# A schedule in pairs for the image parts of a four-layer model on one core, with some of its evictions moved between engines

## The chip, the core and the metric

The kernel runs on one core of one Trainium2 chip. The metric is device time in microseconds (us), the median over runs. The kernel before takes 21348.91 us (three runs, 21327.56 to 21384.39).

## The reference

Eight images of 56 x 56 pixels and 192 channels pass through four residual layers in float32; each layer normalizes its input by groups first (`_gn`).

```python
def _gn(v, G=32, eps=1e-5):
    ...
x = x + _L0_conv_ref(_gn(x), ...)   # gated Toeplitz products along rows and columns
x = x + _L1_conv_ref(_gn(x), ...)   # attention in shifted windows of 7 x 7, 6 heads of 32
x = x + _L2_conv_ref(_gn(x), ...)   # depthwise 3 x 3 convolution
x = x + _L3_conv_ref(_gn(x), ...)   # selective scan in four directions
```

The core of each:

```python
# layer 0
p, q, v = silu(x @ p_w.T + p_b), silu(x @ q_w.T + q_b), silu(x @ v_w.T + v_b)
out = (p * (toeplitz_rows(q * v) + toeplitz_columns(q * v))) @ o_w.T + o_b
# layer 1
attn = softmax(q * scale @ k.T + bias + mask); out = (attn @ v) @ proj_w.T + proj_b
# layer 3: DI = 384 channels, N = 16 states, K = 4 directions, L = 3136 positions
xi, z = split(x @ in_proj_w.T); xc = silu(depthwise_conv(xi)); z = silu(z)
dts, Bs, Cs = split(einsum('bkdl,kcd->bkcl', xs, x_proj_w))
delta = softplus(einsum('bkrl,kdr->bkdl', dts, dt_w) + delta_bias)
h[l] = exp(delta[l] * A) * h[l-1] + delta[l] * u[l] * B[l];  y[l] = sum over N of h[l] * C[l] + D * u[l]
out = (layernorm(sum over the directions of y) * z) @ out_proj_w.T
```

## The kernel before

**Ahead of the loop.** Some 3290 us prepare everything: the products q * v of layer 0 for all images, the Toeplitz products along both axes, and the whole *front* of image 0.

**A front** is what one image needs before its scan can run. It is a Python generator that calls five stages in order: `gate` (the rest of layer 0: the projection p with its Silu, transposes on TensorE, the output projection), `attention` (layer 1), `conv2` (layer 2), `inner` (layer 3's input projection, its convolution and its Silu) and `steps` (the projections to delta, B and C). Each `yield` ends a *piece*, a short run of instructions; the yield says how many PSUM banks the piece holds, how many the next one needs, and after which time a load will have landed. A front has 1144 pieces.

**The loop of pairs.** The scan is cut into chunks of 448 positions. A chunk has three blocks of 128 channels and 16 states, taken two states at a time: a *pair*. An image has 4 directions x 7 chunks x 3 x 8 = 672 pairs; all images, 5376. The order is written out by hand (`manual_schedule`). For one pair: GpSimd multiplies delta * u by B into a ring buffer (`inject`, L1102); ScalarE computes exp(delta * A) into a double-buffered PSUM tile ps_a (`decay`, L1119, two instructions); VectorE scans (`scan`, L1128); GpSimd (even pairs) or VectorE (odd pairs) multiplies by C into one of four hc buffers (`times_c`, L1134); TensorE adds up over the states in PSUM (`add_up`, ps_y, L1149); ScalarE copies a few columns of state (L1109, L1141). Once in eight pairs VectorE adds ps_y into ysum (`sums`, L1159 and L1161).

**Front beside scan.** While image b is scanned, `Parts.step`, called once per pair, resumes pieces of the front of image b + 1, and of `finish` (layer 3's normalization and output for chunks that are complete). The planner keeps an estimated time for each engine (`self.t`) and the estimated cost of every piece, logged by `Meter` when a piece first runs, from fixed prices per instruction and column. `fits` lets a piece in if, by these estimates, VectorE would not have to wait more than 0.2 us for its input and ScalarE and TensorE stay below limits that depend on the next scans. A piece that doesn't fit waits for the next pair, and each such wait adds 3 us to what it is allowed:

```python
t, at, grace = dict(self.t), entry.ready, 3.0 * entry.waits
for engine, cost in entry.costs[entry.at]:
    if engine == "D" and at > t["D"] + limit["D"] + grace:
        return False
    at = t[engine] = max(t[engine], at) + cost
return all(t[e] <= max(limit[e] + grace, self.t[e]) for e in "AE")
```

So a front goes ahead as fast as it fits, and the next front is added as soon as the last one is done. There is one point at which it is forced: before the first chunk of the next image is loaded (16 pairs before the image's end), the planner drains the front until the delta of that chunk has been made (`made`).

All pieces of fronts and of finish share two PSUM banks (`bank`, tile ps_f), the scan has the others. Every engine runs its instructions in the order in which they were put in, and so does the DMA queue on SyncE, which carries nearly all transfers.

**What the change touches in `attention` and `steps`.** In `attention`, for every quarter of a row of windows, the scores of heads 4 and 5 and the values v share one PSUM bank: ScalarE copies v out (L688) and VectorE reads the scores with scale and bias (`biased`, L662); a reduction for the maximum follows (L691), then the exponentials (L694) and a reciprocal (L699). In `steps`, for each of 14 chunks and 3 channel blocks, two banks hold delta for the two directions of a scan order; ScalarE evicts both with their bias (L976), and then takes the Softplus of the whole chunk with its table loads (L980, L428).

Other lines that are named below: L546 to L566 belong to `gate`, L823 to L835 are conv2's convolution and its evictions, L854 loads the rows for inner's convolution, L912 is that convolution and L922 its eviction, L961 and L971 are the matmuls of `steps`. In the first execution of a front (for image 0) all lines appear as L83, the helper that records the costs.

Of the kernel before, what the change touches and what calls it, by code (L numbers as in the profile page):

```python
# [17 lines left out]
ALU = mybir.AluOpType  # L18
# [21 lines left out]
WP = W + 2  # L40
RUN = 8 * WP
SLOT = NG * (CH + 1) + HALF


class Meter:
# [43 lines left out]
def model(ctx: ExitStack, tc: tile.TileContext, a: dict, out: bass.AP):  # L89
# [300 lines left out]
    with (  # L390
# [44 lines left out]
        nc.vector.tensor_reduce(Dsum, Ds, axis=AX.X, op=ALU.add)  # L435


        meter, costs = Meter(tc.nc), {}
        made = set()


# [129 lines left out]
        def attention(b):  # L571
# [52 lines left out]
            for wh in range(H // WS):  # L624
# [27 lines left out]
                for q in range(4):  # L652
                    kind = 2 * (wh == 7) + (q == 3)

                    def scores(p, hh, t):
                        row = slice(hh * HD, (hh + 1) * HD)
                        nc.tensor.matmul(
                            p[:PT_, t * PT_ : (t + 1) * PT_], qk[row, t, q, :], qk[row, 2 + t, q, :], start=True, stop=True
                        )

                    def biased(p, hh):
                        nc.vector.scalar_tensor_tensor(  # L662
                            S[:, 2 * hh : 2 * hh + 2, :],
                            p[:PT_, : 2 * PT_].rearrange("p (t m) -> p t m", t=2),
                            HD**-0.5,
                            bmask[:, kind, 2 * hh : 2 * hh + 2, :],
                            ALU.mult,
                            ALU.add,
                        )


                    yield 0, 2
                    p0, p1 = bank(), bank()
                    for t in range(2):
                        scores(p0, 0, t)
                        scores(p1, 1, t)
                    yield 2, 0
                    biased(p0, 0)
                    biased(p1, 1)
                    yield 0, 1  # L680
                    p = bank()
                    for t in range(2):
                        scores(p, 2, t)
                    pv = p[:PT_, 2 * PT_ : 2 * PT_ + C]
                    for k in range(2):
                        nc.tensor.matmul(pv, xw[:, k, q, :], w_qkv[:, k, 2 * C :], start=k == 0, stop=k == 1)
                    yield 1, 0
                    nc.scalar.copy(v, pv)  # L688
                    biased(p, 2)
                    mx, sm = mxs[:, 0], mxs[:, 1]  # L690
                    nc.vector.tensor_reduce(mx, S, axis=AX.X, op=ALU.max, negate=True)  # L691
                    yield 0, 0
                    for e in range(6):
                        nc.scalar.activation(  # L694
                            S[:, e, :], S[:, e, :], AF.Exp, bias=mx[:, e : e + 1], accum_out=sm[:, e : e + 1]
                        )
                        if e == 2:
                            yield 0, 0
                    nc.vector.reciprocal(sm, sm)  # L699
                    yield 0, 0  # L700
                    for e in range(6):
                        nc.scalar.activation(S[:, e, :], S[:, e, :], AF.Copy, scale=sm[:, e : e + 1])  # L702
                        if e == 2:
                            yield 0, 0
                    for g in range(2):
                        yield 0, 1
                        p = bank()
                        for e in range(3):
                            nc.tensor.transpose(  # L709
                                p[:PT_, e * PT_ : (e + 1) * PT_], S[:, 3 * g + e, :], ident[:PT_, :PT_]  # L710
                            )
                        yield 1, 0
                        nc.scalar.copy(
                            ST[:, 3 * g : 3 * g + 3, :].rearrange("p a m -> p (a m)"), p[:PT_, : 3 * PT_]
                        )
                    yield 0, 1
                    p = bank()
                    for t in range(2):
                        for hh in range(3):
                            h = 3 * t + hh  # L720
                            nc.tensor.matmul(
                                p[hh * HD : (hh + 1) * HD, t * PT_ : (t + 1) * PT_],
                                v[:, h * HD : (h + 1) * HD],
                                ST[:, 2 * hh + t, :],
                                start=True,
                                stop=True,
                            )
                    yield 1, 0
                    nc.scalar.copy(oT[:, :, q, :], p[:CP, : 2 * PT_].rearrange("p (t m) -> p t m", t=2))
# [212 lines left out]
        def steps(b):  # L942
# [11 lines left out]
            for n, (o, j) in enumerate(todo):  # L954
                tok = slice(j * CH, (j + 1) * CH)
                if n + 1 < len(todo):
                    load_x(n + 1)
                yield 0, 1
                p = bank()
                for d in range(ND):  # L960
                    nc.tensor.matmul(p[:, :CH], w_x[:, o, d, :], xc[:, n % 2, d, :], start=d == 0, stop=d == ND - 1)  # L961
                yield 1, 0
                nc.scalar.copy(rc[:, n % 2, :], p[:, :CH])
                nc.sync.dma_start(out=bc_d[o][b][:, tok], in_=rc[64:, n % 2, :])
                for d in range(ND):
                    yield 0, 2
                    held = []
                    for s in range(2):
                        row = slice(32 * s, 32 * s + R)
                        held.append(bank())  # L970
                        nc.tensor.matmul(  # L971
                            held[s][:, :CH], w_dt[row, o, d * 128 : (d + 1) * 128], rc[row, n % 2, :], start=True, stop=True
                        )
                    yield 2, 0
                    for s in range(2):
                        nc.scalar.activation(  # L976
                            dl[:, s, d, :], held[s][:, :CH], AF.Identity, bias=dt_b[:, 2 * o + s, d : d + 1]
                        )
                yield 0, 0
                nc.scalar.activation(dl, dl, AF.Softplus)  # L980
                usual_functions()
                for s in range(2):
                    nc.sync.dma_start(out=dl_d[2 * o + s][b][:, :, tok], in_=dl[:, s])
                made.add((b, o, j))
            yield 0, 0

        def front(b):
            yield from gate(b)
            yield from attention(b)
            yield from conv2(b)  # L990
            yield from inner(b)
            yield from steps(b)

        def finish(b, j):

# [168 lines left out]
        class Parts:  # L1164
# [4 lines left out]
            def __init__(self):  # L1169
                self.clients = []  # L1170
                self.t = dict.fromkeys("PADE", 0.0)

            def run(self, engine, cost, *after):
                self.t[engine] = max(self.t[engine], 0.0, *after) + cost
                return self.t[engine]

            def add(self, work, name):
                entry = Entry(work, costs.setdefault(name, []))
                self.clients.insert(0 if name != "front" else len(self.clients), entry)
                return entry  # L1180

            def fits(self, entry, limit):
                if entry.at >= len(entry.costs):
                    return True
                t, at, grace = dict(self.t), entry.ready, 3.0 * entry.waits
                for engine, cost in entry.costs[entry.at]:
                    if engine == "D" and at > t["D"] + limit["D"] + grace:
                        return False
                    at = t[engine] = max(t[engine], at) + cost
                return all(t[e] <= max(limit[e] + grace, self.t[e]) for e in "AE")  # L1190

            def resume(self, entry):
                got = log_of(entry.work, entry.costs) if entry.at == len(entry.costs) else next(entry.work, None)
# [10 lines left out]
            def step(self, limit, only=None):  # L1204
                old = [e for e in self.clients if e.held]
                for entry in old + [e for e in self.clients if e not in old]:
                    if only is not None and entry is not only and not entry.held:
                        continue
                    while entry in self.clients:
                        if entry.held and entry not in old:  # L1210
                            break
                        if entry.needs + sum(e.held for e in self.clients if e is not entry) > 2:
                            break
                        if not self.fits(entry, limit):
                            entry.waits += 1
                            break
# [3 lines left out]
                        self.resume(entry)  # L1220

        class Entry:
            def __init__(self, work, costs):
                self.work, self.costs = work, costs
                self.at = self.held = self.needs = self.waits = 0
                self.ready = 0.0

# [32 lines left out]
        with tc.manual_schedule():  # L1260
# [31 lines left out]
            ending, anything = None, dict.fromkeys("ADE", 1e9)  # L1292
            for g, (i, d, k) in enumerate(pairs):
                b, slot, j = chunks[i]
                if ahead_of not in parts.clients and b_next < B:
                    ahead_of = parts.add(front(b_next), "front")
                    b_next += 1
# [53 lines left out]
                times_c(last)  # L1351
            for g in (last - 1, last):
                add_up(g)
            while parts.clients:
                parts.step(anything)
            sums(i, d)
# [105 lines left out]
```

## Time and profile before

| | |
|---|---|
| median of the runs | 21348.91 us (21327.56 to 21384.39) |
| profiled execution, its own time | 21337.26 us |
| its span on the core | 21335.4 us |
| mean granted TensorE clock | 0.885 |
| first to last scan of the loop (L1128) | 3288 to 21296 us |
| gate to steps of the front of image 4 | 10065 to 12310 us |
| scan (L1128), mean of one | 2.02 us |
| GpSimd's inject (L1102) and times_c (L1134), mean of one | 1.77 us |
| VectorE's times_c (L1134), mean of one | 1.09 us |
| one exponential of ScalarE (L1119) | 0.64 us |
| eviction of delta by ScalarE (L976), mean of one | 0.63 us |

The profile is of one execution. PE is TensorE (matmuls), PEld its weight loads, DVE VectorE, ACT ScalarE, POOL GpSimd, SP SyncE. Busy times are summed over instructions; matmuls overlap, so a busy PE is not a full one. A row such as "DVE hc L1134 <- PE ps_y L1149" in the list of waits says that the VectorE instruction of line 1134 that writes hc was ready to go but for the TensorE instruction of line 1149, with the total, the number of times and the longest wait in us.

### The profile page before, as it was taken

What the parts mean: (1) busy time and instruction counts of PE and PEld (TensorE: products, weight loads), DVE (VectorE), ACT (ScalarE), POOL (GpSimd) and SP (SyncE); (2) the same over time, 40 slices, a digit from 0 to 9 for tenths busy, and PEclk for the clock granted to TensorE, in tenths of its full rate; (3) what the DMA queues carried; (4) which work ended last, traced back from release to release, by engine and by line L of the source; (5) the groups of instructions that cost most, each with busy time, mean ns of one, the idle gap of its engine ahead of it and who ended that gap; (6) DMA issues with size and microseconds to landing.
All of it is one profiled execution on the core that took longest, in us unless ns stands there. A gap on an engine that the chain in (4) does not pass through costs nothing. (4 is left out here: it accounts for less than half of the span.)

```text
span 21335.4 us, 204096 instructions
## 1 busy us (share of the span) xinstructions
PE 17278.2 (81%) x59420; PEld 8930.3 (42%) x59420; DVE 15942.8 (75%) x12633; ACT 12339.9 (58%) x31627; POOL 15616.3 (73%) x9378
## 2 busy tenths in 40 slices
PE   8878658878887788878987898879877987787777
PEld 4666524433443344433543354335433443333333
DVE  2432207986798679977897779867987789689998
ACT  3111235766666666757675757666666666575555
POOL 1222206977888778867897778878887788699999
PEclk9988768988998889888998899889988999888888
DMA  4776565456545655475546654565447544754444
GB/s 99 180 179 161 123 189 158 135 171 206 168 135 152 214 160 150 127 205 188 151 138 182 206 154 134 167 210 169 145 138 219 174 143 136 218 177 147 135 133 128
DMA packets 2562886, 3470.49 MB, mean 163 GB/s; under 512 B 932463, under 2 KB 2514897, under 8 KB 2530931
## 3 DMA queue, kind: packets, MB, share of 16 engines
q1 hardware_dynamic: 2456772, 3253.90, 51.3%
q10 hardware_dynamic: 86016, 86.71, 1.8%
q0 software_dynamic: 18976, 116.82, 1.6%
q8 instruction: 473, 7.75, 0.2%
q14 instruction: 649, 5.31, 0.1%
HBM read 2822.68 MB, written 634.11 MB: 162 GB/s over the span
## 5 line engine op out<-in xcount | busy, mean ns | idle before, releaser
L1149 PE MATMUL ps_y<-hc,ident_sb 128*128 128x448 f32 x21504 | 9984.7, 602 | 831.0 <-POOL hc L1134 757.0
L1102 POOL TENSOR_TENSOR ring<-du,bm 128x896 f32<-128x896 f32 x5376 | 9438.2, 1770 | 723.1 <-ACT ring L1109 367.5
L1119 ACT ACTIVATE ps_a<-delta,A_logs_sb 128x449 f32<-128x449 f32 x10752 | 6859.4, 638 | 357.1 <-DVE ring L1128 100.5
L1149 PEld LDWEIGHTS ps_y<-hc,ident_sb 128*128 128x128 f32 x21504 | 4308.3, 210 | 5153.0 <-issue 3638.6
L1134 POOL TENSOR_TENSOR hc<-ring,cm 128x896 f32<-128x896 f32 x2688 | 4757.6, 1770 | 2013.9 <-DVE ring L1128 991.2
L1128 DVE TENSOR_TENSOR_SCAN ring<-ps_a,ring 128x898 f32<-128x898 f32 x2688 | 5423.3, 2018 | 826.0 <-ACT ps_a L1119 719.9
L1128 DVE TENSOR_TENSOR_SCAN ps_a<-ps_a,ring 128x898 f32<-128x898 f32 x2688 | 5426.9, 2019 | 612.1 <-ACT ps_a L1119 552.9
L1134 DVE TENSOR_TENSOR hc<-ps_a,cm 128x896 f32<-128x896 f32 x2688 | 2934.4, 1092 | 1017.2 <-PE ps_y L1149 789.8
L1141 ACT COPY state<-ps_a 128x2 f32<-128x2 f32 x2687 | 425.9, 159 | 2813.2 <-DVE hc L1134 2805.1
L279 POOL COPY tm<-tr 112x2688 f32<-112x2688 f32 x96 | 458.7, 4800 | 1117.2 <-DMA tr<-ext 646.7
L1109 ACT COPY ring<-state 128x2 f32<-128x2 f32 x4608 | 822.9, 179 | 516.8 <-POOL hc L1134 515.9
L312 PE MATMUL ps_tz<-tzx,tm 112*112 112x112 f32 x4608 | 927.1, 370 | 189.2 <-POOL tm L279 181.1
L1085 POOL TENSOR_TENSOR du<-delta,xcd 128x448 f32<-128x448 f32 x672 | 657.0, 978 | 496.8 <-DMA xcd<-xc 496.8
L312 PEld LDWEIGHTS ps_tz<-tzx,tm 112*112 112x112 f32 x4608 | 870.5, 202 | 238.6 <-POOL tm L279 189.1
L316 DVE COPY tzx<-ps_tz 112x448 f32<-112x448 f32 x576 | 356.4, 622 | 744.6 <-PE ps_tz L312 705.2
L709 PE MATMUL ps_f<-ident_sb,slab 98*98 98x98 f32 x1344 | 336.9, 324 | 596.2 <-ACT slab L702 596.0
L1141 ACT COPY state<-ring 128x2 f32<-128x2 f32 x2688 | 504.2, 188 | 474.6 <-DVE ring L1128 459.5
L83 PE MATMUL ps_f<-slab 96*32 96x448 f32 (+7 forms) x2432 | 600.2, 554 | 166.7 <-DMA slab<-pad 76.2
L241 ACT ACTIVATE sl<-ps_qv 128x384 f32<-128x384 f32 x600 | 293.0, 490 | 755.7 <-PE ps_qv L240 612.1
L242 DVE TENSOR_TENSOR qv<-sl 128x576 f32<-128x576 f32 (+1 forms) x200 | 206.8, 1037 | 572.5 <-ACT sl L241 556.6
L709 PEld LDWEIGHTS ps_f<-ident_sb,slab 98*98 98x98 f32 x1344 | 200.9, 155 | 1009.3 <-ACT slab L702 794.2
L546 PE MATMUL ps_f<-ident_sb,slab 112*96 112x112 f32 x4704 | 538.4, 270 | 98.8 <-DVE slab L554 46.3
(223 smaller groups left out, 16977.5 us busy)
## 6 DMA issues: line engine op xcount, KB each, us to landing
bm<-bc SPq DMA_DIRECT2D x1792, 448.0 KB
cm<-bc SPq DMA_DIRECT2D x1792, 448.0 KB
xcd<-xc SPq DMA_DIRECT2D x840, 224.0 KB
dl<-slab SPq DMA_DIRECT2D x224, 672.0 KB
delta<-dl SPq DMA_DIRECT2D x224, 672.0 KB
slab<-pad SPq DMA_DIRECT2D x504, 232.0 KB
o<-tzx POOLq DMA_DIRECT2D x192, 588.0 KB, 12.8
slab<-x SPq DMA_DIRECT2D x280, 336.0 KB
```

The costliest lines, as they stand in the source:

```text
L83: return f(*args, **kw)
L312: nc.tensor.matmul(po[:, c, :], t[:, c2 + c, :], x[:, :, c1 + c2 + c], start=True, stop=True)
L546: nc.tensor.matmul(p[:CP, t * TT : (t + 1) * TT], ot[:, n % 2, i, t, c % 2 * CP : c % 2 * CP + CP], ident[:TT, :TT], start=i == 0, stop=i ...
L709: nc.tensor.transpose(p[:PT_, e * PT_ : (e + 1) * PT_], S[:, 3 * g + e, :], ident[:PT_, :PT_])
L1085: nc.gpsimd.tensor_mul(du[:, 0, :], deltas[i][:, d, 1 : CH + 1], xcs.pop((i, d)))
L1102: nc.gpsimd.tensor_mul(hs[:, :, tokens(i)[0]], dus[i, d].to_broadcast([128, NG, CH]), bms[i, k])
L1109: nc.scalar.copy(in_ring(g)[:, :, tokens(i)[1]], src)
L1119: nc.scalar.activation(dA[:, n, :], deltas[i][:, d, at : at + CH + 1], AF.Exp, scale=negA[:, slot, d, c : c + 1])
L1128: nc.vector.tensor_tensor_scan(h, dA, hs, 0.0, ALU.mult, ALU.add)
L1134: (nc.gpsimd if on_pool(d, k) else nc.vector).tensor_mul(hc, h[:, :, tokens(i)[0]], cms[i, k])
L1141: nc.scalar.copy(states[i][:, d, NG * k : NG * k + NG], h[:, :, tokens(i)[2]])
L1149: nc.tensor.matmul(yps[i, d][:, :CH], ident, hcs[g][:, n, :], start=k + n == 0, stop=k + n == NP + NG - 2)
```

## The change

The change has three parts.

1. The fronts follow a schedule counted in pairs. `PER_FRONT = 676` pairs are given to a front. `shares` divides them among the pieces: for each stage it sums the logged costs by engine, weights them by `ROOM` (pairs per us of TensorE, VectorE and ScalarE work), takes the largest of the three sums or a third of the number of pieces as the stage's share, and splits that among its pieces by their weighted cost. `late` is the number of pairs by which a front is behind its schedule. A front's piece that holds no bank isn't resumed while the front is more than 1.5 pairs ahead, and its grace in `fits` is its lateness (not below zero) in place of 3 us per wait. Pieces that hold a bank, and those of `finish`, keep the old rule.
2. Of the two banks of delta in `steps`, ScalarE evicts the first as before, and VectorE the second (`tensor_scalar`, adding the bias).
3. In `attention`, `biased(p, 2)` on VectorE is issued ahead of ScalarE's copy of v from the same bank.

```diff
+ROOM = {"E": 0.8, "D": 2.2, "A": 0.7}
+PER_FRONT = 676
...
                     yield 1, 0
+                    biased(p, 2)
                     nc.scalar.copy(v, pv)
-                    biased(p, 2)
...
                     yield 2, 0
-                    for s in range(2):
-                        nc.scalar.activation(
-                            dl[:, s, d, :], held[s][:, :CH], AF.Identity, bias=dt_b[:, 2 * o + s, d : d + 1]
-                        )
+                    nc.scalar.activation(dl[:, 0, d, :], held[0][:, :CH], AF.Identity, bias=dt_b[:, 2 * o, d : d + 1])
+                    nc.vector.tensor_scalar(
+                        dl[:, 1, d, :], held[1][:, :CH], dt_b[:, 2 * o + 1, d : d + 1], None, ALU.add
+                    )
...
         def front(b):
-            yield from gate(b)
-            yield from attention(b)
-            yield from conv2(b)
-            yield from inner(b)
-            yield from steps(b)
+            log = costs["front"]
+            for stage in (gate, attention, conv2, inner, steps):
+                if b == 0:
+                    stages.append(len(log))
+                yield from stage(b)
+
+        def shares():
+
+            log, at, share = costs["front"], stages + [len(costs["front"])], []
+            for lo, hi in zip(at, at[1:]):
+                sums = [{e: sum(c for f, c in piece if f == e) * per for e, per in ROOM.items()} for piece in log[lo:hi]]
+                whole = max(len(sums) / 3, *(sum(piece[e] for piece in sums) for e in ROOM))
+                total = sum(sum(piece.values()) for piece in sums)
+                share += [whole * sum(piece.values()) / total for piece in sums]
+            done = [0.0]
+            for v in share:
+                done.append(done[-1] + v / sum(share))
+            return done
...
             def __init__(self):
                 self.clients = []
                 self.t = dict.fromkeys("PADE", 0.0)
+                self.pair, self.done, self.fronts = 0, shares(), -1
...
             def add(self, work, name):
-                entry = Entry(work, costs.setdefault(name, []))
+                entry = Entry(work, costs.setdefault(name, []), name == "front")
+                self.fronts += entry.paced
...
                 t, at, grace = dict(self.t), entry.ready, 3.0 * entry.waits
+                if entry.paced and not entry.held:
+                    grace = max(0.0, self.late(entry))
...
+            def late(self, entry):
+                return self.pair - PER_FRONT * (self.fronts + self.done[entry.at])
...
                         if entry.needs + sum(e.held for e in self.clients if e is not entry) > 2:
                             break
+                        if entry.paced and not entry.held and only is None and self.late(entry) < -1.5:
+                            break
                         if not self.fits(entry, limit):
...
             for g, (i, d, k) in enumerate(pairs):
                 b, slot, j = chunks[i]
+                parts.pair = g
```

More of the change, by code (lines that the diff above doesn't have):

```diff
@@ L435, in model @@
         nc.vector.tensor_reduce(Dsum, Ds, axis=AX.X, op=ALU.add)
-        meter, costs = Meter(tc.nc), {}
+        meter, costs, stages = Meter(tc.nc), {}, []
         made = set()
@@ L1222, in model, with __init__ @@
         class Entry:
-            def __init__(self, work, costs):
-                self.work, self.costs = work, costs
+            def __init__(self, work, costs, paced):
+                self.work, self.costs, self.paced = work, costs, paced
                 self.at = self.held = self.needs = self.waits = 0
@@ L1353, in model @@
                 add_up(g)
+            parts.pair = 2 * len(pairs)
             while parts.clients:
```

## The prediction

> **What bounds the kernel now.** I read the page first for the busy shares, then cut the span into the stages of one image's front, because the 21 ms hold regimes with different limits.
>
> ```profile
> PE 17278.2 (81%) x59420; PEld 8930.3 (42%) x59420; DVE 15942.8 (75%) x12633; ACT 12339.9 (58%) x31627; POOL 15616.3 (73%) x9378
> DVE  2432207986798679977897779867987789689998
> POOL 1222206977888778867897778878887788699999
> ```
>
> No engine is full on the mean. In the 40 slices GpSimd and VectorE are full only in the last five or so, where no front is left; before that they rise and fall with the image. The page's chain of waits covers too little of the span to say more. So: busy time by stage for the front of image 4 (gate, attention, conv2, inner, steps, in order), and last a stretch of image 7 with no front beside it.
>
> ```profile
> 10065.00:10561.00 496.00, 453.61 (x1732) 260.66 (x1731) 409.07 (x314) 284.96 (x659) 396.14 (x240) 0.96 0.58 161
> 10561.00:11344.00 783.00, 651.60 (x2337) 321.13 (x2335) 738.41 (x614) 572.88 (x1804) 704.98 (x421) 0.91 0.42 130
> 11344.00:11513.00 169.00, 111.08 (x408) 40.91 (x408) 132.13 (x121) 67.67 (x174) 104.17 (x62) 0.84 0.62 171
> 11513.00:11932.00 419.00, 326.40 (x1138) 143.15 (x1138) 296.11 (x188) 253.32 (x563) 309.36 (x184) 0.86 0.74 226
> 11932.00:12310.00 378.00, 313.09 (x787) 141.63 (x788) 267.13 (x173) 283.73 (x570) 285.61 (x173) 0.85 0.58 189
> 19600.00:20800.00 1200.00, 872.62 (x1770) 373.51 (x1769) 1148.39 (x722) 670.68 (x1775) 1198.49 (x720) 0.87 0.41 135
> ```
>
> The columns are length, then PE, PEld, DVE, ACT, POOL. The same windows for the scan's line (one scan is one pair) give 138, 258, 39, 114 and 100 pairs, and 444 in the last. Without a front a pair takes 1200/444 = 2.70 us, GpSimd is full and VectorE is busy 1148/444 = 2.59 us of it. A front's 649 pairs take 2245 us where 649 x 2.70 = 1754 would do: 491 us extra. I split that by VectorE. Its own front work (busy less 2.59 per pair) is 52, 71, 31, 1 and 9 us, 164 in all. The rest is its idle time beyond the 0.116 per pair of the free stretch: gate 71, attention 14, conv2 32, inner 110, steps 99, together 326 us. That idle is what a schedule can win. What ends it, by the waits over the whole stretch of the fronts (us in total, times, longest), and then over conv2's 169 us:
>
> ```profile
> DVE hc L1134 <- PE ps_y L1149: 779.0, 480, 11.1
> DVE ps_a L1128 <- ACT ps_a L1119: 513.5, 313, 10.0
> DVE ring L1128 <- ACT ps_a L1119: 408.0, 150, 4.6
> ```
>
> ```profile
> DVE slab L834 <- PE ps_f L823: 33.3, 11, 10.3
> ```
>
> First, VectorE waits for TensorE to free an hc buffer; second, for ScalarE's exponentials. Both engines run in order, so a front's piece that waits holds the pairs up. One case, in order of time:
>
> ```profile
> 4714.05 4.16 PE L912 MATMUL ps_f<-slab 96*32 96x448 f32 x24 [4.23 <-DMA slab<-pad]
> ...
> 4719.94 1.09 DVE L1134 TENSOR_TENSOR hc<-ps_a,cm 128x896 f32<-128x896 f32 x1 [6.64 <-PE ps_y L1149]
> ```
>
> The inner convolution was put into TensorE's queue before its rows had landed; the sums behind it came late, and VectorE stood for 6.6 us.
>
> **The schedule.** The shares follow from the planner's prices (its bookkeeping, not chip times). Gate: 84 projections and 84 output matmuls at 0.60 and 336 transposes at 0.18 make 161 TensorE us, x 0.8 = 129.5. Attention: 559 pieces / 3 = 186. conv2: 25.6 VectorE us x 2.2 = 56. Inner: 108 TensorE us x 0.8 = 86. Steps, with half the evictions moved: 104.7 ScalarE us x 0.7 = 73. Sum 531.7, scaled to 676 pairs: 165, 237, 71, 110, 93, against 138, 258, 39, 114, 100 now. So only gate and conv2 get room; the other three are asked to run slightly denser than they run unpaced. Before, the last front ends at pair 4534 of 5376 (stage positions counted against scans); paced it ends near 7 x 676 = 4732, still with a free last image.
>
> Gate: its 71 us of idle scaled with density, 71 x 138/165 = 59: -12 us a front. TensorE is busy 454 of 496 us here, so density is what hurts.
> Attention: 14 x 258/237 = 15: +1.
> conv2: 33.3 us of its idle is one wait, the eviction at L834 for a convolution that waits for padded rows. By the prices the 14 convolutions come about 3.4 pairs apart instead of little over one, so rows ordered two ahead have some 19 us to land. I take 28 of the 32 us off.
> Inner: the convolution's share is 1.9 pairs a step against about 1.4 now; of the 54.6 us that VectorE waits there for ps_y I take a fifth, -11; the rest at 114/110 gives +4. Net -7.
> Steps: 99 x 100/93 = 106: +7.
> Grace: a piece that doesn't fit gets 3 us more for each pair it waits; a paced one gets its lateness instead. Behind a load of 8 us the old rule issues after one pair, the new one after two if the front is on time. About eleven such waits a front stall TensorE or VectorE; each can win up to one pair (2.7 us) or, when the front is late by 6 or more, lose as much. So between -30 and +30; I take -10, since gate and conv2 leave it on time and the others don't.
>
> **Delta's banks.** 42 of 84 evictions a front leave ScalarE and come to VectorE, with no DMA moved.
>
> ```profile
> L976 ACT ACTIVATE slab<-ps_f,dt_b_sb 128x448 f32<-128x448 f32 x84 | 48.6, 627 | 21.3 <-PE ps_f L971 21.1
> L316 DVE COPY tzx<-ps_tz 112x448 f32<-112x448 f32 x576 | 356.4, 622 | 744.6 <-PE ps_tz L312 705.2
> ```
>
> ScalarE loses 42 x 0.627 = 26 us. VectorE has no such operation; its reads of a bank of 448 columns cost 0.595 (L1161) to 0.677 (L834), so 25 to 28 us, and I take L316's 0.61 to 0.62: 26. In steps VectorE waits for ScalarE 42 of its 111 idle us, so ScalarE's relief is worth 0.38 x 26 = 10; of VectorE's 26, what falls ahead of an idle gap is free, and I count half, 13. Net +3, between -10 and +26. Behind each added instruction stand the next scan and hc; if TensorE is late, they wait too, and the Softplus of 2.4 us with its two table loads of 1.28 now waits for VectorE.
>
> The Trainium skill (Perfetto Trace Analysis, Optimizing Scalar/DVE Operations) speaks against this move: it gives VectorE some 125 ns of access overhead on PSUM and ScalarE 51, and would move work off a saturated VectorE. By its figures 294 moved evictions would cost 22 us more on VectorE than they save on ScalarE. The rows above show no such gap, so the sum goes by the rows.
>
> **The shared bank.** VectorE now reads the score bank (0.35 us) before ScalarE copies v (0.32 us). All that VectorE waits for the copy in the whole trace is 12.8 us (13 waits). Now ScalarE waits instead, at most 0.35 us x 224 = 78 us in all if nothing covers it; it is busy 573 of 783 us in attention, and the exponentials that follow need the maximum from VectorE anyway. I take 0, between -13 and +78. The Trainium skill (PSUM — Partial Sum Buffer, PSUM bank collisions) says that two engines, even two readers, must be kept off one bank, so one of them will always wait.
>
> **The sum.** -12 + 1 - 28 - 7 + 7 - 10 + 3 = -46 us a front, x 7 = -322. The profiled execution took 21337 us, 12 below the median: 21015 there, about 21025 as a median.
>
> **Rivals.** *It costs time*, by lateness in attention. It takes 258 pairs unpaced and is given 237; if it can't, lateness builds up, and lateness is grace for every piece, so VectorE's reciprocals are issued before ScalarE's exponentials are done and the scans stand behind them. Attention now idles VectorE 5.7%; if that rose to gate's (496 - 409)/496 = 17.5%, it would cost 0.118 x 783 x 237/258 = 85 us a front. With the -46 that is +39, x 7 = +273: 21620. It decides from about 46 us a front, an idle share of 12%. For it: three stages of five get denser. Against it: those 258 pairs came with a grace of 3 us for each wait, and one or two late pairs give as much. The forced drain at the first delta chunk isn't the risk: that chunk falls due near pair 590 and is needed at 656, a margin of 66, shrinking by 4 a front to 42.
>
> *The schedule is a wash*: conv2 and gate win 40, and steps, now always under the finishing work of the image before, give it back. 21290 to 21410.
>
> *A large gain*: if smaller grace also takes half of the idle in inner and steps (209/2 = 104 a front), the sum is about -150 a front, -1050: 20300; with a third of that idle, -116 a front, 20540.
>
> **How the numbers follow.** Forecast 42%, centre 21025, its own range 20800 to 21280 (the lower bounds of grace and evictions together are -33 us a front from the centre, the upper ones +63, of which I keep somewhat over half, since the whole would need a late front throughout and no cover at all). Large gain 18%, wash 10%, costs time 30%. Within 0.3% (64 us, about what a measurement of this kernel can tell from no change) is the wash alone: faster 60%, same 10%, slower 30%. The range leaves out a tenth at either end: 20480 to 21620.
>
> **What would show it.** Right: conv2 spread over some 71 pairs with the wait of L834 for L823 nearly gone; gate near 165 pairs; the last front ending near pair 4732; VectorE busy some 180 us more in all, ScalarE as much less; waits for ps_y down. Wrong: more idle in attention, before the reciprocal above all; steps running past its share with lateness carried into the next gate; the added evictions waiting for L971; or pairs in inner and steps clearly below the 3.7 us of now, which would be the large gain.

## The result, and the profile after

The changed kernel takes 21457.56 us (median of five runs, 21450.69 to 21468.90) against 21357.99 for the kernel before in the same comparison: a ratio of 1.0048, 95% interval 1.0033 to 1.0063. It is slower, by 0.5%. The forecast was a gain of 1.5%; the range held the time, the sign was wrong.

The page of the changed kernel, busy time by engine and the two rows of the 40 slices (line numbers are some three higher in attention, sixteen higher in the loop):

```profile
PE 17218.9 (80%) x59420; PEld 8970.6 (42%) x59420; DVE 16141.0 (75%) x12969; ACT 12207.4 (57%) x31291; POOL 15611.9 (73%) x9378
DVE  2432208886898779887888689877988688868998
POOL 1222208886788778887888788877888788878999
```

VectorE does 198 us more than before and ScalarE 133 less. The slices still rise and fall with the image, and the full stretch without a front has shrunk from five slices to some three: the last front now ends at pair 4736, before at 4534. The stages of the fifth front, and a stretch of the last image with no front beside it, in the columns and order of the prediction:

```profile
12648.00:13162.00 514.00, 465.89 (x1699) 259.12 (x1698) 468.96 (x345) 303.50 (x720) 447.08 (x267) 0.95 0.58 162
13162.00:13962.00 800.00, 633.29 (x2280) 318.27 (x2278) 696.73 (x590) 556.06 (x1746) 665.30 (x396) 0.88 0.39 119
13962.00:14171.00 209.00, 151.04 (x513) 61.09 (x513) 199.26 (x163) 107.08 (x278) 173.47 (x103) 0.85 0.67 194
14171.00:14626.00 455.00, 350.06 (x1264) 164.62 (x1264) 301.54 (x198) 269.57 (x599) 327.16 (x198) 0.88 0.72 220
14626.00:14997.00 371.00, 300.74 (x821) 142.11 (x821) 277.59 (x209) 259.71 (x518) 273.31 (x167) 0.91 0.60 195
19900.00:21000.00 1100.00, 802.60 (x1626) 345.81 (x1625) 1054.39 (x663) 614.35 (x1629) 1099.83 (x661) 0.87 0.41 135
```

The scan's line has 163, 244, 65, 114 and 94 instructions in the five stages and 408 in the last window, so the free pace is still 1100/408 = 2.70 us. Gate and conv2 are now nearly full of VectorE work (469 of 514, 199 of 209). Attention is not: 697 of 800, where before it was 738 of 783. The waits of VectorE over the stretch of the fronts name what is new there:

```profile
DVE hc L1150 <- PE ps_y L1165: 574.2, 344, 14.1
DVE mxs L702 <- ACT slab L697: 522.0, 224, 2.6
DVE ps_a L1144 <- ACT ps_a L1135: 493.3, 242, 11.5
DVE ring L1144 <- ACT ps_a L1135: 331.3, 117, 13.6
```

The waits for ps_y fell by 205 us and those for the exponentials of the scan by 97. But the reciprocal of the softmax now stands before ScalarE's exponentials in each of its 224 executions, 2.3 us a time. Before, it was this row:

```profile
DVE mxs L699 <- ACT slab L694: 139.8, 183, 0.9
```

The trace can be cut at the first instruction of each stage, for all seven fronts. A stage's length less 2.70 us for each pair in it is its extra cost; the table has it in us per front (pairs in brackets). The last columns are the extra after the last front (the tail), the loop from first to last scan, and its start.

| kernel | gate | attention | conv2 | inner | steps | tail | loop | start |
|---|---|---|---|---|---|---|---|---|
| before | 113 (138) | 91 (259) | 60 (39) | 120 (114) | 104 (98) | 81 | 18006 | 3288 |
| changed | 72 (163) | 142 (243) | 37 (65) | 149 (113) | 116 (92) | 42 | 18163 | 3248 |

The five stages cost 28 us more a front, 196 in all; the tail costs 39 less, since one fewer finish stands alone there, and the loop starts 40 us earlier: 196 - 39 - 40 = 117, and the spans of the two traces differ by 115. A table of this kind compares single executions: the traced one of the kernel before took 21337.26 us, and its median in the comparisons below is 21357.99 to 21377.65, so a difference of 20 to 40 us between the whole spans of two traces says little.

### The profile page after: what moved, and what is told of

It reads as the page before. It is cut to its first block, busy times and chain, and to the rows that moved or that the text cites. A ratio compares the mean times of both kernels' runs of the same rounds, so it can differ in the third digit from the quotient of the medians.

```text
span 21450.0 us, 204780 instructions
## 1 busy us (share of the span) xinstructions
PE 17218.9 (80%) x59420; PEld 8970.6 (42%) x59420; DVE 16141.0 (75%) x12969; ACT 12207.4 (57%) x31291; POOL 15611.9 (73%) x9378
## 5 line engine op out<-in xcount | busy, mean ns | idle before, releaser
L86 PE MATMUL ps_f<-slab 96*32 96x448 f32 (+7 forms) x2432 | 624.5, 580 | 176.6 <-DMA slab<-pad 96.7
L549 PEld LDWEIGHTS ps_f<-ident_sb,slab 112*96 112x96 f32 x4704 | 540.5, 178 | 365.3 <-issue 204.7
## 6 DMA issues: line engine op xcount, KB each, us to landing
o<-tzx POOLq DMA_DIRECT2D x192, 588.0 KB, 12.8
```

The source lines that it names most:

```text
L86: return f(*args, **kw)
L549: nc.tensor.matmul(p[:CP, t * TT : (t + 1) * TT], ot[:, n % 2, i, t, c % 2 * CP : c % 2 * CP + CP], ident[:TT, :TT], start=i == 0, stop=i ...
```

## The experiments

Below, the swap is the change in the order of the two readers of the score bank, and the moves are the swap and delta's second bank on VectorE. Theory G: lateness used as grace lets attention's reciprocals in before their exponentials are done, and lateness comes from a share too small. Its rivals, taken up as the runs came: S, the swap makes the reciprocal late; W, the swap disturbs the planner, not the engines; P, the schedule pins the finishing work on inner and steps, and that costs what the rest wins.

**The grace of VectorE's pieces alone.**

```diff
-                    if engine == "D" and at > t["D"] + limit["D"] + grace:
+                    if engine == "D" and at > t["D"] + limit["D"] + 3.0 * entry.waits:
```

> Edit: the changed kernel, but a piece with a VectorE instruction gets the old grace (3 us for each pair that it has waited) for VectorE's readiness; ScalarE and TensorE keep lateness as grace. Theory G (lateness as grace lets the reciprocals in before the exponentials are done): the 75 us of waiting before the reciprocal in one front's attention fall to about 18 as before, attention gets a few pairs longer, and the time falls by some 7 x 45 to 57 us, to 21060 to 21150. Theory S (the reciprocal waits because the swap holds ScalarE's copy of v back): the waits stay at 60 us or more and the time stays within 60 us of 21458.

Measured: 21587.98 us, ratio 1.0103 (1.0088 to 1.0118). A miss for both. The wait before the reciprocal:

```profile
DVE mxs L702 <- ACT slab L697: 336.7, 224, 2.6
```

It fell by a third only. Attention took 274 pairs, its extra fell from 142 to 124, and the delay came out of conv2, which went back to 35 pairs and from 37 to 68 us of extra. Mending one wait made the front later (followed through the planner's own bookkeeping, 20 pairs late at the reciprocals on the mean, against 7 in the changed kernel), and lateness stayed the grace of the other engines.

**Both moves without the schedule.** The edit is the diff's two moves on the kernel before.

> Edit: the kernel before with both moves (delta's second bank and the score bank first on VectorE) and no schedule. Theory G: the moves alone are near neutral, reciprocal waits stay near 18 us a front, time within 100 us of 21358. Theory S: reciprocal waits rise to 60 us or more a front and the time rises by 200 us or more.

Measured: 21443.10 us, 1.0034 (1.0021 to 1.0047). The reciprocals' wait is 105.8 us in the whole trace, so S is out as the main cause: without the schedule the wait is no longer than before. But the moves aren't neutral. Attention took 320 pairs with hardly any idle (in the fifth front VectorE was busy 890 of 929 us), and from the second front on steps began at pair 656 of the image: the point at which the planner drains the front by force. Inner cost 197 us a front.

**The schedule without the moves.**

> Edit: the changed kernel with the schedule alone; both moves undone. Theory G: the reciprocal waits stay at 60 to 80 us a front and the time stays at 21400 to 21560. Theory S: the waits fall to about 20 us a front and the time falls to 21050 to 21150.

Measured: 21514.10 us, 1.0063 (1.0043 to 1.0082).

```profile
DVE mxs L702 <- ACT slab L697: 461.3, 196, 2.6
DVE mxs L702 <- ACT state L1157: 65.4, 28, 2.3
```

In the other 28 executions the profile names the small copy of the state that stands on ScalarE at that place. Together it is 527 us, and attention costs 152 a front in 232 pairs. The reciprocals' wait belongs to the schedule, as G says.

**The schedule with the old grace, both moves kept.**

```diff
-                if entry.paced and not entry.held:
-                    grace = max(0.0, self.late(entry))
```

> Edit: the changed kernel with the old grace for every piece; the schedule only holds back a front that is ahead. Theory G: reciprocal waits near 18 us a front, attention back at some 258 pairs, gate and conv2 keep their gain (idle 45 and 10 us a front); time 21000 to 21150, at or below the run with the old grace for VectorE alone. Theory P (inner and steps lose because the finishing work now falls on them): inner's extra stays at some 150 us a front here too, against 111 before. Theory S: no gain in attention, time above 21350.

Measured: 21473.48 us, 1.0051 (1.0036 to 1.0066). The reciprocals' wait went (105.3 us), and the time did not: attention took 321 pairs, as with the moves alone, gate was back at 135 pairs and conv2 at 39, and steps ran into the forced drain. The time lies where S put it, above 21350, but not for S's reason, since the wait that S would explain is gone. So taking lateness away, with the rest of the change in place, changes the time little (21457.56 with it): one loss went and another came, neither G nor P can be read here, and something in the moves stretches attention. The next runs take them one by one.

**The swap alone.**

> Edit: the kernel before with the swap of the score bank alone. Theory W (the swap makes the planner hold that piece back for a pair or more in every quarter of a window row, because its chain of estimates now goes VectorE, ScalarE, VectorE): attention grows from 259 to some 320 pairs a front with almost no idle in it, steps start at the forced point (pair 656 of the image) from the third front on, inner costs 60 to 90 us a front more, and the time is 21450 to 21560. Rival (the swap only moves a wait of at most 0.35 us between two engines): attention stays at 255 to 265 pairs and the time within 64 us of 21366.

Measured: 21519.89 us, 1.0067 (1.0050 to 1.0085). Attention and inner of the fifth front:

```profile
13282.00:14214.00 932.00, 765.98 (x2593) 376.71 (x2592) 893.93 (x718) 669.29 (x2060) 878.28 (x525) 0.92 0.41 129
14392.00:14851.00 459.00, 339.25 (x1237) 161.64 (x1236) 258.58 (x169) 247.48 (x528) 278.46 (x169) 0.83 0.66 201
```

Attention takes 932 us for 322 pairs, with VectorE busy 894 us of it: a smooth stage, but ten pairs to a quarter of a window row where before there were eight. Inner then has 94 pairs and VectorE is busy 259 of 459 us. Followed through its own bookkeeping, the planner now refuses the swapped piece once in each of the 224 quarters, and the piece with the reciprocal in each too, always because VectorE would wait; in the kernel before, it refuses the one twice in all and the other 58 times. W holds so far: a change of two lines in the order of issue costs 142 us, with pieces let in at other pairs.

**Delta's banks alone.**

> Edit: the kernel before with half of delta's banks on VectorE alone. Theory W (all of the moves' loss is the swap's): the loop starts some 40 to 60 us earlier, because ahead of the loop the first front's steps are bound by ScalarE, the stages keep their pairs, steps cost 0 to 15 us a front less, and the time is 21210 to 21330. Rival (VectorE's new instructions cost what they take): 0 to 60 us above 21366.

Measured: 21310.47 us, 0.9968 (0.9954 to 0.9982), 67 us faster. The loop starts at 3286, so the early start expected here isn't delta's; the start at 3255 in the run before shows that it is the swap's. The medians show the 67 us; the two traces differ by 12 us only, and the five stages by 3 us a front, so where the gain lies is open.

**The schedule that only holds back, with delta's move.** The old grace as above, and the swap undone.

> Edit: the changed kernel without the swap and with the old grace for all pieces, so the schedule only holds back a front that is ahead. Theory G (the loss is lateness used as grace, which the swap makes worse): attention at 259 pairs with some 16 us idle a front, gate near 72 us above the free pace, inner and steps together no worse than with the change (265 us above it); time 21050 to 21200. Theory P (the fixed phase against the finishing work costs what the schedule wins): inner and steps together 40 us a front or more above the 223 of before, time 21250 to 21400.

Measured: 21315.80 us, 0.9970 (0.9959 to 0.9981). Attention costs 88 us a front in 258 pairs, gate 73, conv2 57, as G has it; inner and steps together 272, as P has it, and the time is outside G's window and in P's.

**The schedule that only holds back, alone.**

> Edit: the schedule that only holds back (old grace for all pieces), and neither move; against the run with the schedule alone it differs in the grace only. Theory G: the idle before the reciprocals falls from 527 us to 100 to 150 in all, attention from 152 to about 91 us a front above the free pace, time 21514 less some 300, 21150 to 21270. Theory P: attention gains that, but the time stays at 21300 to 21450, since inner and steps stand as they do with the change.

Measured: 21229.19 us, 0.9930 (0.9915 to 0.9945): the fastest of all kernels here. Against the schedule alone (21514.10) only the grace differs, and it is worth 285 us. The wait before the reciprocal:

```profile
DVE mxs L702 <- ACT slab L697: 136.5, 188, 0.9
```

Attention fell from 152 to 86 us a front; gate stays at 71 (150 pairs). This is G, with its price.

**The swap in the old plan.** The kernel before with the swap, and the planner's cost record of that piece put back in the old order, so that every piece lands where it did.

```diff
+            if [e for e, _ in meter.log] == ["D", "A", "D"]:
+                meter.log[:2] = meter.log[1::-1]
             log.append(meter.log)
```

> Edit: the kernel before with the swap, and the planner's logged costs of that one piece put back in the old order (ScalarE, VectorE, VectorE), so that every piece lands at the pair where it lands in the kernel before, and only the two readers of the bank change places. Theory W (the swap's loss is the planner's): attention at 259 pairs, the loop within 30 us of before's 18006, and what the swap saves ahead of the loop, some 30 to 50 us, stays: 21310 to 21380. Rival (the bank order itself costs): attention's extra rises by 10 us a front or more and the time is above 21440.

Measured: 21374.30 us, 1.0001 (0.9992 to 1.0010). All stages keep their pairs, attention 259. So the 142 us of the swap alone came from the plan. The time is in W's window, but not for W's reason only: the loop is 91 us longer, not within 30, and it starts 53 us earlier. Attention costs 11 us a front more, as the rival had it. The 38 us left between the two traces are not in the medians, since the traced execution of the kernel before is 39 us faster than its median here. So S has a small part in it after all. The wait before the reciprocal, now that ScalarE's copy of v comes after VectorE's reading, and the wait of that copy, which the kernel before doesn't have:

```profile
DVE mxs L699 <- ACT slab L694: 220.2, 221, 1.3
ACT slab L689 <- DVE slab L662: 519.2, 223, 4.7
```

The first is 80 us longer than before, 11 us a front: what attention lost.

**Both: hold back, swap in the old plan.** Lateness is no grace, delta stays on ScalarE.

> Edit: the schedule that only holds back (old grace), with the swap and the old cost order for its piece, delta left on ScalarE. Theory W: the run that only holds back (21229) less what the swap saves ahead of the loop: 21170 to 21230. Rival (the bank order itself costs): above 21260.

Measured: 21278.04 us, 0.9956 (0.9944 to 0.9969), slower than holding back alone. Attention costs 96 us a front in place of 86, with 216.5 us of waits before the reciprocals in place of 136.5; the loop starts 52 us earlier and is 84 longer. The rival's threshold of 21260 was passed: in the loop the old order of the two readers is better.

**Room for attention, lateness kept as grace.**

```diff
-                whole = max(len(sums) / 3, *(sum(piece[e] for piece in sums) for e in ROOM))
+                whole = max(len(sums) / 2.45, *(sum(piece[e] for piece in sums) for e in ROOM))
```

> Edit: the schedule alone with lateness as grace, as in the run with the schedule alone, but attention's share counts a pair for 2.45 pieces in place of 3, which gives it 261 of the 676 pairs, what it takes unpaced. Theory G (the loss is lateness, and lateness comes from a share that is too small): by the planner's own books lateness in attention falls from several pairs to under one; the idle before the reciprocals falls from 527 to 130 to 250 us, attention's extra from 152 to 85 to 100 us a front, and the time from 21514 to 21180 to 21300. Rival (the new grace is worse than the old one whatever the share): reciprocals' idle stays above 400 us and the time above 21400.

Measured: 21290.15 us, 0.9960 (0.9948 to 0.9973). The new grace is kept, and the reciprocals' wait is near that of the kernel before (139.8):

```profile
DVE mxs L702 <- ACT slab L697: 179.2, 197, 2.6
```

Attention costs 90 us in 259 pairs, and by the planner's bookkeeping the front is 0.6 pairs late at the reciprocals on the mean, where with the schedule alone it was 3.3. The share is the cause, and grace the way in which it costs. The room came from inner, which costs 162 in 103 pairs.

**Holding back at 650 pairs.** `PER_FRONT = 650`, otherwise the schedule that only holds back.

> Edit: the run that only holds back (old grace, neither move), with 650 pairs to a front in place of 676, so the fronts drift ahead as in the kernel before and the finishing work falls on gate and attention instead of inner and steps; hardly a piece is held back. Theory P (the fixed phase costs): inner and steps fall to 118 and 57 to 120 us a front, gate stays near 75, and the time is 21100 to 21200, below 21229. Rival (finishing costs about the same wherever it falls): gate rises to 110 us a front or more by as much as inner and steps fall, and the time returns to 21320 to 21400, so that holding back is what won.

Measured: 21351.41 us, 0.9991 (0.9982 to 1.0000). The fronts drift ahead, the finishing work moves onto gate, and gate rises from 71 to 100 us a front while inner and steps together fall from 265 to 237. Finishing costs about the same wherever it falls; P is out. What is lost against 676 pairs is 122 us, spread over the stages and the tail.

## Why the prediction was wrong

**The steps that failed.** *Attention: +1.* Its idle was scaled with density, as if stalls only spread. It measured +51 us a front (142 against 91). The reciprocals' wait accounts for all of it: 522 - 140 = 382 us over seven fronts, 55 each. *Grace: -10, between -30 and +30.* I looked for it at loads, where a front on time would wait a pair longer. It acted where the front was late, on every piece at once: without the moves, where it was taken alone, it cost 285/7 = 41 us a front, outside the bounds. With them the swap hides that price: the changed kernel takes 21457.56 us with lateness as grace and 21473.48 without, and only with the swap gone too, 21315.80. In the trace lateness can be counted: conv2 was due at pair 401.5 of the first front and begins at 412, some ten pairs late, and ten pairs are 10 us of grace. Followed through its own bookkeeping, the planner lets VectorE wait 1.7 us on the mean at a reciprocal, where before it was 0.1. The old rule gave 3 us for a wait, and only to the piece that had waited.

*The shared bank: 0, between -13 and +78.* Three errors. The wait of 12.8 us was taken from the lines of attention; the front of image 0 runs under the helper's line (L83, in the changed kernel L86), and there VectorE's waits for ScalarE's writes and copies were ten times as long, 121.9 of 127.3 us of them at its readings of the scores. Before, and then changed:

```profile
DVE slab L83 <- ACT slab L83: 127.3, 25, 19.5
```

```profile
DVE slab L86 <- ACT slab L86: 8.3, 3, 4.4
ACT slab L692 <- DVE slab L665: 188.6, 222, 3.1
```

This wait of the first front is 5 to 13 us in all seven kernels with the swap, which start the loop at 3231 to 3255, and 125 to 129 in all seven without it, which start it at 3280 to 3302. It is the likely source of the earlier start; that the one sets the other was not tested by itself. Second, ScalarE's new wait isn't the 0.35 us of the reading but up to 3.1: 188.6 us against a bound of 78, and 519.2 in the run that keeps every piece at its place. A scan and a product of VectorE take 2.02 and 1.09 us, so the copy seems to stand behind these as well as behind the reading. And the prediction's sentence that one of the two will always wait was too strong for the old order: VectorE waited for the copy 13 times in 224. Third, and largest, I priced the swap on the engines and not in the planner. Its estimates run through a piece as a chain, and with VectorE, ScalarE, VectorE the second VectorE instruction seems to come late by the copy (0.36 by the planner's prices, 0.2 allowed). In its bookkeeping this check refuses the piece in each of the 224 quarters, in the swap alone and in the changed kernel. That the recorded order is what costs the 142 us is shown by the run that puts it back.

**Steps that held, or held by accident.** conv2: -28 forecast, -23 measured; 65 pairs, and the eviction's wait for the convolution, 33 us in one front before, isn't among VectorE's waits in the changed kernel's conv2 (fifth front):

```profile
DVE gn_st L792 <- DMA slab<-x: 8.8, 4, 8.0
DVE hc L1150 <- PE ps_y L1165: 3.7, 1, 3.7
DVE ps_a L1144 <- ACT ps_a L1135: 1.4, 1, 1.4
```

Gate -12, inner -7, steps +10 measured -41, +29 and +12: wrong one by one, and right in sum (-9 forecast, 0 measured), because all three are one thing that I had split by stage: the finishing work left gate for inner and steps, and the run at 650 pairs moves it back at about the same cost. Free of it, gate was near 72 us with the first front before, too (pairs 3 to 134), so the "71 us of idle" of gate were mostly finish. Start and tail, -79 us together, were in no step.

Delta's banks: +3 us a front forecast, -67 in all measured alone, just inside the bounds (-70 to +182 for seven fronts). The unit cost was off:

```profile
L979 DVE TENSOR_SCALAR slab<-ps_f,dt_b_sb 128x448 f32<-128x448 f32 x294 | 198.4, 675 | 61.1 <-PE ps_f L974 36.6 <-DMA dl<-slab 23.9
L978 ACT ACTIVATE slab<-ps_f,dt_b_sb 128x448 f32<-128x448 f32 x294 | 184.8, 629 | 143.1 <-PE ps_f L974 132.1 <-DMA dl<-slab 10.8
```

VectorE takes 0.675 us where ScalarE takes 0.629, at the upper end of the rows, not at the copy's 0.622. The page of the Trainium skill named in the prediction has the two engines' overheads on PSUM 74 ns apart; the two instructions measure 46 ns apart, so its direction was right and the row that the sum went by was not. Its advice is for a saturated VectorE, and this one is busy 75% of the span: alone, the move was worth 67 us by the medians. With the schedule that only holds back the kernel that has it is the slower one (21315.80 against 21229.19); why is open, and the two ran in one comparison.

**The rivals.** "It costs time, by lateness in attention" named the mechanism and the instruction. Its price was 85 us a front; measured are 51, and the sum of the five stages +28 against its +39. It got 30% because the 258 pairs of attention were taken for something that a little more grace would shorten. They were shortened, in the way that the rival named and at some 60% of its price, and nothing in the profile of before spoke for a cheap way. The wash, by finishing work under steps, was the wrong reason: that work costs the same elsewhere.

## What to carry to other kernels

A planner that lets work in by estimated readiness can turn a number used as slack into stalls on in-order engines: keep lateness out of the readiness test, or give each stage the share that it takes unpaced. When two instructions change places, follow the change through the scheduler's own estimates as well as on the engines, and look for the same wait under every line that can carry it, helpers included. Before stage costs are compared, take out work that merely moved between them.

## What the hardware showed that was not expected

When two engines read one PSUM bank one after the other, what the second waits for can be far longer than the first one's reading. VectorE's reading of the scores takes 0.34 us; with every piece at its place and VectorE first, ScalarE's copy waited 519.2 us in 223 waits, 2.3 us on the mean and up to 4.7, and in the changed kernel 0.85 us on the mean and up to 3.1. The Trainium skill (PSUM — Partial Sum Buffer, PSUM bank collisions) has the rule that keeps the two apart, so that one can have to wait; the runs add what the choice is worth here: some 10 us a front in attention for ScalarE first, and some 50 us ahead of the loop for VectorE first.
